# Attention and expert layer on one core: the experts' second product moved behind the two-level rounds

## The chip, the cores and the metric

The kernel runs on one core of a Trainium2 chip. The metric is the device time of one execution in microseconds; the median of several runs counts. The engines of the core are TensorE (PE), VectorE (DVE), ScalarE (ACT), GpSimd (POOL) and SyncE (SP), whose queue issues all DMAs of this kernel.

## The reference, cut to what matters

```python
x = hidden_states                                    # (2, 512, 512), float32
xn = layernorm(x)
out = x + attn(xn) + ffn(xn)

# attn: linear attention with decay, 32 heads of 128, over xn
#   q, k, v = silu(xn @ qkv_w.T);  gate = sigmoid(xn @ gate_w.T)
#   result  = (gate * rmsnorm(scan(q, k, v)) * norm_w) @ out_w.T

# ffn over the 1024 tokens of xn
logits  = xn @ W_router.T                            # 8 experts
combine = top-2 of softmax(logits), renormalised     # (1024, 8)
h       = einsum('nd,erd->ner', xn, A)               # rank 16 for each expert
hw      = h * combine[:, :, None]
ffn     = xn @ W_base.T + b_base + einsum('ner,eor->no', hw, B) * 2
```

What the change concerns is the last line: the base projection `xn @ W_base.T`, the bias, and the experts' second product with `B` (called `wlb` in the kernel, 128 rows of expert and rank by 512).

## The kernel before, in words

The 1024 tokens are eight tiles of 128 (NT = 8, four for each of the two sequences). Everything is float32. The kernel has these stages.

**Setup.** The eight tiles of x are loaded and normalised in four groups (L240 to L260). For each tile PE transposes xn into `xnT` (L252, bank "fr", copied by ACT at L253), multiplies it with the router and the experts' first weights (`wra`, bank "ra"), and ACT copies the logits `lg` and the experts' inner values `hl`. `base(t)` (L227) projects tile t with `wbase` into one of four banks `seeded` (sd0 to sd3, tile t uses t mod 4), and DVE adds the result to `x_sb[t]` (L233); it is called three tiles behind the transposes. Then DVE finds the two best experts of every token (L266 to L299) and scales `hl` by their weights (L300), forms the sums `xsum` of blocks of `xnT` (L306 to L309) and the second-level sums `xt` (L316 to L319). POOL adds the bias to `x_sb` (L321). PE transposes `hl` (L326), ACT copies it (`hT`, L329), PE multiplies with `wlb` (L333, recorded at the helper's line L80), DVE adds to `x_sb[t]` (L334), and the sum is stored in DRAM as `x_kept`.

**Two-level rounds.** The products that give v and the gate for all heads are done by a fast matrix multiplication scheme with seven products at two levels. `rounds` lists the outer products (n, q), seven for each of eight sets of weights n (four of v, four of the gate); each has seven inner products, whose slots are in `SLOTS`, two of them trailing one round behind. POOL makes the operands two rounds ahead: `encode` builds outer sums `s` (L177, a pool of 5 buffers) and inner sums `e` (L191 to L194, 3 buffers) from the raw weights. PE multiplies (L362, L366) into banks "fr" and the four `seeded`; DVE and ACT combine (L401 to L434) through temporaries of the pool `aw2` (`temp`: `z` with 6 buffers, `c` with 2); finished blocks go to DRAM (`v_kept`, `gate_kept`).

**First phase.** For each head the products for q and k (L488, one level), the attention (L550 to L589), and stores of gated heads.

**Second phase.** The output projection, in one level, with the first three pairs already worked in at the end of the first phase; at the end `x_kept` is read back, and the rows are finished and stored.

The order of the instructions on every engine is not written out by hand: a scheduler places the program's instructions in the engines' queues, and semaphores follow from the tiles. An engine works its queue in order. A pool's buffer is given out again when the last reader of its earlier tile is done. The pools `sp` (setup) and `aw2` share memory, as do the pools of the rounds and those of the first phase. The phase's PSUM banks ("ch", "sc", "at") take over the banks of the rounds.

Of the kernel before, what the change touches and what calls it, by code (L numbers as in the profile page):

```python
# [33 lines left out]
F32 = mybir.dt.float32  # L34
AF = mybir.ActivationFunctionType
ALU = mybir.AluOpType
# [4 lines left out]
P = 128  # L41
B, S, HID = 2, 512, 512
# [3 lines left out]
NT = B * TB  # L46
# [3 lines left out]
NE, R = 8, 16  # L50
# [9 lines left out]
def attn_moe_kernel(ctx: ExitStack, tc: tile.TileContext, x, qk_w, v_w, gate_w, out_w, norm_w,  # L60
                    decay, base_w, base_b, router_a_w, lora_b, out):
    nc = tc.nc
# [6 lines left out]
    dram = pool("dram", DRAM)  # L69
# [6 lines left out]
    def bank(tag):  # L76
        return ps.tile([P, 512], F32, tag=tag, name=f"ps_{tag}", bufs=banks[tag])

    def mm(o, lhsT, rhs, start, stop):
        nc.tensor.matmul(o, lhsT, rhs, start=start, stop=stop)  # L80
# [10 lines left out]

    v_kept, gate_kept = ([dram.tile([P, 2, HG, B, S], F32, tag=f"{n}_kept{i}", name=f"{n}_kept{i}")
                          for i in range(NG // 2)] for n in ("v", "gate"))
    x_kept = dram.tile([P, NT, HID], F32, tag="x_kept", name="x_kept")

    def inv_sqrt(sp, mean_sq, n, name, scale=None):

# [75 lines left out]
    def encode(n, q):  # L173

        def outer(k, a, b, op):
            t = sums2[n, k] = aw.tile([P, 2, 2, 256], F32, tag="s", name="s", bufs=5)
            nc.gpsimd.tensor_tensor(t, a, b, op)  # L177

        if q == 6:
            outer(1, raw_block(n, 1, 0), raw_block(n, 1, 1), ALU.add)  # L180
            outer(2, sums2[n, 1], raw_block(n, 0, 0), ALU.subtract)
        elif q == 7:
            outer(3, raw_block(n, 0, 0), raw_block(n, 1, 0), ALU.subtract)
        elif q == 3:
            outer(4, raw_block(n, 0, 1), sums2[n, 2], ALU.subtract)
        block = {1: lambda: raw_block(n, 0, 0), 2: lambda: raw_block(n, 0, 1), 3: lambda: sums2[n, 4],
                 4: lambda: raw_block(n, 1, 1), 5: lambda: sums2[n, 1], 6: lambda: sums2[n, 2],
                 7: lambda: sums2[n, 3]}[q]()
        a11, a12, a21, a22 = (inner(n, block, i, j) for i in range(2) for j in range(2))
        e = aw.tile([P, 4, 2, P], F32, tag="e", name="e", bufs=3)  # L190
        nc.gpsimd.tensor_tensor(e[:, 0], a21, a22, ALU.add)  # L191
        nc.gpsimd.tensor_tensor(e[:, 1], e[:, 0], a11, ALU.subtract)
        nc.gpsimd.tensor_tensor(e[:, 2], a11, a21, ALU.subtract)
        nc.gpsimd.tensor_tensor(e[:, 3], a12, e[:, 1], ALU.subtract)  # L194
        operand[n, q] = {1: a11, 2: a12, 3: e[:, 3], 4: a22, 5: e[:, 0], 6: e[:, 1], 7: e[:, 2]}

    rounds = []
# [3 lines left out]
    rounds.append((NSET - 1, 4))  # L201


    xt = [aw.tile([P, 4, S // 2], F32, tag=f"xt{q}", name=f"xt{q}") for q in range(1, 8)]
    with tc.tile_pool(name="setup", bufs=1) as sp:
        x_sb = [sp.tile([P, HID], F32, tag=f"x{t}", name=f"x{t}") for t in range(NT)]
# [1 line left out]
        nc.gpsimd.memset(ones, 1.0)  # L208
        wra = sp.tile([P, KC, NE + ER], F32, tag="wra", name="wra")
        wbase = sp.tile([P, KC, HID], F32, tag="wbase", name="wbase")  # L210
        wlb = sp.tile([P, HID], F32, tag="wlb", name="wlb")
        bias = sp.tile([P, HID], F32, tag="bias", name="bias")
        for t in range(NT):
            nc.sync.dma_start(x_sb[t], x[t * P : (t + 1) * P, :])
            if t == 2:
                nc.sync.dma_start(wra, router_a_w)
        nc.sync.dma_start(wbase, base_w)
        nc.sync.dma_start(bias, base_b.partition_broadcast(P))
        nc.sync.dma_start(wlb, lora_b)
        load_set(0)  # L220
        nc.sync.dma_start(nw, norm_w)
        load_set(1)
# [4 lines left out]
        def base(t):  # L227

            b, tt = divmod(t, TB)
            bp = seeded[t % 4]  # L230
            for c in range(KC):
                mm(bp, xnT[b][:, c, tt * P : (tt + 1) * P], wbase[:, c, :], c == 0, c == KC - 1)
            nc.vector.tensor_tensor(x_sb[t], x_sb[t], bp, ALU.add)  # L233


        lg = sp.tile([P, NT, NE], F32, tag="lg", name="lg")
        hl = sp.tile([P, NT, NE, R], F32, tag="hl", name="hl")
        stats = sp.tile([P, NT, 6], F32, tag="stats", name="stats")
        mv = sp.tile([P, NT, 2], F32, tag="mv", name="mv")
        for g, ts in enumerate(((0,), (1, 2), (3, 4, 5), (6, 7))):  # L240
            for t in ts:
                nc.vector.bn_stats(stats[:, t, :], x_sb[t])
                nc.vector.bn_aggr(mv[:, t, :], stats[:, t, :])
            rstd = inv_sqrt(sp, mv[:, ts[0] : ts[-1] + 1, 1], len(ts), f"ln{g}")
            for i, t in enumerate(ts):
                b, tt = divmod(t, TB)
                xn = sp.tile([P, HID], F32, tag="xn", name="xn", bufs=4)
                nc.vector.tensor_scalar(xn, x_sb[t], mv[:, t, 0:1], rstd[:, i : i + 1],
                                        ALU.subtract, ALU.mult)
                tp = bank("fr")  # L250
                for c in range(KC):
                    nc.tensor.transpose(tp[:, c * P : (c + 1) * P], xn[:, c * P : (c + 1) * P], ident)  # L252
                nc.scalar.copy(xnT[b][:, :, tt * P : (tt + 1) * P],  # L253
                               tp.rearrange("p (c s) -> p c s", c=KC))
                ra = bank("ra")
                for c in range(KC):
                    mm(ra[:, : NE + ER], xnT[b][:, c, tt * P : (tt + 1) * P], wra[:, c, :],
                       c == 0, c == KC - 1)
                nc.scalar.copy(lg[:, t, :], ra[:, :NE])
                nc.scalar.copy(hl[:, t].rearrange("p e r -> p (e r)"), ra[:, NE : NE + ER])  # L260
                if t > 2:
                    base(t - 3)
        for t in range(NT - 3, NT):
            base(t)

        prio = sp.tile([P, NT, NE], F32, tag="prio", name="prio")  # L266
        for e in range(NE):
# [50 lines left out]
            nc.vector.tensor_tensor(t[:, 2], i22, i12, ALU.subtract)  # L318
            nc.vector.tensor_tensor(t[:, 3], i21, t[:, 1], ALU.subtract)  # L319
        for t in range(NT):  # L320
            nc.gpsimd.tensor_tensor(x_sb[t], x_sb[t], bias, ALU.add)  # L321

        for q in range(NT // 4):
            tp = bank("fr")
            for i in range(4):
                nc.tensor.transpose(tp[:, i * P : (i + 1) * P],  # L326
                                    hl[:, q * 4 + i].rearrange("p e r -> p (e r)"), ident)
            hT = sp.tile([P, 4 * P], F32, tag="hT", name="hT", bufs=2)
            nc.scalar.copy(hT, tp)  # L329
            for i in range(4):  # L330
                t = q * 4 + i
                lp = seeded[i]
                mm(lp, hT[:, i * P : (i + 1) * P], wlb, True, True)  # L333
                nc.vector.tensor_tensor(x_sb[t], x_sb[t], lp, ALU.add)  # L334
                nc.sync.dma_start(x_kept[:, t, :], x_sb[t])

# [12 lines left out]
    def temp(tag, bufs=2):  # L351
        return aw2.tile([P, 512], F32, tag=tag, name=tag, bufs=bufs)

    def inner_product(o, r, i, first):
        n, q = rounds[r]
        a = operand[n, q][i]
        x_ = {1: xo[q][:, 0, :HB], 2: xo[q][:, 1, :HB], 3: xo[q][:, 1, HB:], 4: xt[q - 1][:, 3],
              5: xt[q - 1][:, 0], 6: xt[q - 1][:, 1], 7: xt[q - 1][:, 2]}[i]
        for u in range(2):
            if n % 2 == 0:  # L360
                for j in range(2):
                    nc.tensor.matmul(o[:, (2 * u + j) * P : (2 * u + j + 1) * P], x_[:, j * P : (j + 1) * P],  # L362
                                     a[:, u], start=first and u == 0 and j == 0, stop=True,
                                     skip_group_check=True)
            else:
                nc.tensor.matmul(o[:, u * HB : (u + 1) * HB], a[:, u], x_, start=first and u == 0, stop=True,  # L366
                                 skip_group_check=True)
# [18 lines left out]
    def after(r, i):  # L386
# [53 lines left out]
        elif i == 4:  # L440
            out_of(2, st["pd"])

    SLOTS = ((0, 1), (0, 5), (0, 2), (1, 7), (0, 6), (0, 3), (1, 4))
    for k in range(7 * len(rounds) + 7):
        r0, m = divmod(k, 7)
        if m == 0:
            if r0 + 2 < len(rounds):
                encode(*rounds[r0 + 2])
            if r0 < len(rounds):
                n, q = rounds[r0]  # L450
                state_of[r0] = {}
                for _, to in ADDED[q]:
                    if isinstance(to, str):
                        outer_sums[n, to] = aw2.tile([P, 4, 512], F32, tag="sum", name="sum", bufs=4)
                if q == 2 and 0 < n < NSET - 1:
                    load_set(n + 1)
                if (n, q) == (NSET - 1, 2):
                    load_pair(0)
                    for i in range(2):
                        load_unit(i)  # L460
        back, i = SLOTS[m]
        r = r0 - back
        if not 0 <= r < len(rounds):
            continue
        st = state_of[r]
        if i in (1, 5):
            st["pa" if i == 1 else "pc"] = bank("fr")
        inner_product(st[{1: "pa", 2: "pa", 5: "pc", 3: "pc", 6: "pb", 7: "pd", 4: "pd"}[i]], r, i, i in (1, 5))
        after(r, i)
    phase_a.close()  # L470


# [342 lines left out]
```

## Time and profile before

| | us |
|---|---|
| median of 3 runs | 1240.16 (1238.93 to 1240.45) |
| the profiled execution | 1241.71 |
| its span in the profile | 1239.9 |
| mean granted TensorE clock | 0.993 |

Busy in the stages, from the trace (us; PE, DVE, POOL):

| stretch | PE | DVE | POOL |
|---|---|---|---|
| 40 to 50 | 10.0 | 10.0 | 10.0 |
| 50 to 60 | 3.0 | 10.0 | 9.8 |
| 60 to 70 | 4.5 | 9.0 | 4.5 |
| 70 to 80 | 10.0 | 5.2 | 0.0 |
| 100 to 150 | 49.8 | 35.1 | 30.1 |
| 420 to 440 | 18.0 | 10.8 | 2.1 |
| 500 to 800 | 300.0 | 130.6 | 115.1 |

A line of a timeline gives start and length in us, the engine, the line of the kernel, the operation, what it writes and reads, shapes and count; in brackets stands the idle time of the engine before it and who released it. Matmuls in float32 leave two records each. PE's busy time is of records that overlap a little (a record holds the drain of the array too), so a row's length is a little more than what it adds to the row before.

### The profile page before, as it was taken

The numbers are of one execution on the slowest core, as the hardware profiler recorded it, in microseconds if no ns is written. First come the engines' busy times: TensorE is split into PE (matmuls) and PEld (weight loads), VectorE is DVE, ScalarE is ACT, GpSimd is POOL, SyncE is SP. The second block draws the span as 40 slices with busy tenths as digits, with TensorE's granted clock in tenths as the row PEclk, the third lists the DMA queues.
The fourth block names the chain that finished last, engine by engine and source line by source line (L and its number), as shares of the span: only waits on it lengthen the run. The fifth ranks groups of instructions, "written<-read, shape, count | busy, mean of one in ns | idle before, by whom it ended". The sixth has DMA issues, their size and how long they took to land.

```text
span 1239.9 us, 17100 instructions
## 1 busy us (share of the span) xinstructions
PE 1207.4 (97%) x6328; PEld 914.3 (74%) x6328; DVE 629.1 (51%) x1104; ACT 366.1 (30%) x648; POOL 592.8 (48%) x662
## 2 busy tenths in 40 slices
PE   6789999999999999999999999999999999999998
PEld 4369889899899745666666666666666669888887
DVE  5757666766766624444444434444444444455333
ACT  2124444444444422223222222222232332320000
POOL 3926568758756241434433433433333343655552
PEclk9989999999999999999999999999999999999999
DMA  8012543452442353343443443343334333843221
GB/s 315 0 68 75 173 151 121 153 170 96 161 161 103 123 166 91 119 135 112 145 140 103 125 134 102 117 125 118 116 114 128 120 97 108 309 150 122 93 92 52
DMA packets 102706, 158.17 MB, mean 128 GB/s; under 512 B 8800, under 2 KB 68192, under 8 KB 101344
## 3 DMA queue, kind: packets, MB, share of 16 engines
q1 hardware_dynamic: 102624, 157.09, 38.2%
q8 instruction: 50, 0.82, 0.3%
q14 instruction: 32, 0.26, 0.1%
HBM read 102.53 MB, written 54.53 MB: 127 GB/s over the span
## 4 chain that ended last, share of the span: by engine, by line
PE 93%; DVE 5%; issue 1%; ACT 1%; DMA 0%; SPq 0%; DVEq 0%; ACTq 0%
PE ps_ch L488 31%; PE ps_ch L645 9%; PE ps_at L80 8%; PE ps_sc L80 8%; PE ps_fr L362 7%; PE ps_fr L366 7%; PE sd L362 5%; PE sd L366 5%; PE ps_sc L645 4%; PE ps_at L645 2%; PE sd L80 2%; PE ps_sc L550 2%; DVE z L405 1%; DVE sum L405 1%; PE ps_ra L80 1%
## 5 line engine op out<-in xcount | busy, mean ns | idle before, releaser
L488 PE MATMUL ps_ch<-xsum,ws 128*128 128x512 f32 x384 | 180.0, 593 | 0.0
L562 POOL TENSOR_TENSOR qd<-q,mask 128x384 f32<-128x384 f32 x64 | 64.2, 1003 | 219.9 <-PE ps_at L80 214.8
L488 PE MATMUL ps_ch<-xnT,w 128*128 128x512 f32 x256 | 122.2, 600 | 0.8 <-DVE z L405 0.8
L488 PEld LDWEIGHTS ps_ch<-xsum,ws 128*128 128x128 f32 x384 | 68.5, 191 | 63.2 <-issue 63.2
L80 PEld LDWEIGHTS ps_at<-scores,v 128*128 128x128 f32 x512 | 77.4, 192 | 28.0 <-issue 27.7
L126 POOL TENSOR_TENSOR ws<-w 128x256 f32<-128x256 f32 x32 | 23.4, 730 | 154.3 <-DMA w<-in_qk_w 154.3
L503 DVE TENSOR_TENSOR c<-ps_ch,u 128x512 f32<-128x512 f32 x96 | 66.4, 691 | 58.4 <-PE ps_ch L488 58.4
L588 DVE SCALAR_TENSOR_TENSOR gT<-gate,ps_at 128x512 f32<-128x512 f32 x64 | 44.0, 687 | 97.5 <-ACT sq L585 94.5
L645 PE MATMUL ps_ch<-wsum,gsum 128*128 128x256 f32 x384 | 89.1, 379 | 0.0
L80 PE MATMUL ps_at<-scores,v 128*128 128x128 f32 x512 | 88.4, 275 | 0.0
L585 ACT ACTIVATE sq<-ps_at 128x512 f32<-128x512 f32 x62 | 37.0, 597 | 155.2 <-PE ps_at L80 155.1
L586 POOL TENSOR_TENSOR ssq<-ssq,sq 128x512 f32<-128x512 f32 x62 | 79.2, 1278 | 6.5 <-ACT sq L585 6.5
L645 PEld LDWEIGHTS ps_ch<-wsum,gsum 128*128 128x128 f32 x384 | 72.3, 190 | 9.5
L80 PE MATMUL ps_at<-qd,state 128*128 128x128 f32 x384 | 74.2, 275 | 0.0
L80 PEld LDWEIGHTS ps_sc<-v,kd 128*128 128x128 f32 x384 | 52.8, 191 | 28.4 <-issue 28.2
L633 POOL TENSOR_TENSOR wsum<-wo 128x256 f32<-128x256 f32 x32 | 25.3, 790 | 93.0 <-PE ps_ch L645 37.4
L488 PEld LDWEIGHTS ps_ch<-xnT,w 128*128 128x128 f32 x256 | 44.4, 192 | 34.2 <-issue 33.1
L503 DVE TENSOR_TENSOR u<-ps_ch,p 128x512 f32<-128x512 f32 x32 | 22.1, 692 | 91.4 <-PE ps_ch L488 85.5
L80 PE MATMUL ps_sc<-q,k 128*128 128x128 f32 x512 | 67.6, 275 | 0.0
L552 ACT ACTIVATE kd<-ps_sc,mask 128x384 f32<-128x384 f32 x64 | 37.2, 580 | 89.8 <-PE ps_sc L550 89.8
L626 DVE TENSOR_TENSOR gsum<-gated 128x256 f32<-128x256 f32 x32 | 15.1, 470 | 95.2 <-PE ps_sc L645 66.7
L80 PEld LDWEIGHTS ps_sc<-q,k 128*128 128x128 f32 x512 | 62.2, 192 | 0.0
(224 smaller groups left out, 2633.6 us busy)
## 6 DMA issues: line engine op xcount, KB each, us to landing
w<-in_qk_w SPq DMA_DIRECT2D x32, 512.0 KB, 4.1
v_kept<-z SPq DMA_DIRECT2D x64, 256.0 KB, 2.4
gate_kept<-z SPq DMA_DIRECT2D x64, 256.0 KB, 2.4
v<-v_kept SPq DMA_DIRECT2D x64, 256.0 KB, 2.6
gate<-gate_kept SPq DMA_DIRECT2D x64, 256.0 KB, 3.2
g_kept<-gT SPq DMA_DIRECT2D x64, 256.0 KB, 2.5
gated<-g_kept SPq DMA_DIRECT2D x32, 512.0 KB, 3.7
raw<-in_v_w SPq DMA_DIRECT2D x8, 1024.0 KB, 6.6
```

What stands on the lines that cost most here:

```text
L80: nc.tensor.matmul(o, lhsT, rhs, start=start, stop=stop)
L362: nc.tensor.matmul(o[:, (2 * u + j) * P : (2 * u + j + 1) * P], x_[:, j * P : (j + 1) * P], a[:, u], start=first and u == 0 and j == 0, st ...
L366: nc.tensor.matmul(o[:, u * HB : (u + 1) * HB], a[:, u], x_, start=first and u == 0, stop=True, skip_group_check=True)
L488: nc.tensor.matmul(o, a[:, c, :], b[:, c, :], start=first and c == 0, stop=c == 1, skip_group_check=True)
L503: nc.vector.tensor_tensor(o, p, t, ALU.add)
L552: nc.scalar.activation(kd.rearrange("p j d -> p (j d)"), pk[:, : (TB - 1) * P], AF.Copy, scale=mask[:, 0, P - 1 : P])
L562: nc.gpsimd.tensor_tensor(qd, q[:, P:].rearrange("p (j n) -> p j n", j=TB - 1), mask[:, 1, :].unsqueeze(1).to_broadcast([P, TB - 1, P]), A ...
L585: nc.scalar.activation(sq, pa, AF.Square)
L586: nc.gpsimd.tensor_tensor(ssq[b], ssq[b], sq, ALU.add)
L588: nc.vector.scalar_tensor_tensor(gT, gate.pop((head, b)), 1.0, pa, ALU.add, ALU.mult)
L633: nc.gpsimd.tensor_tensor(t[:, 0], b12, b11, ALU.subtract)
L645: nc.tensor.matmul(sums[n][:, i * HO : (i + 1) * HO], l[:, i * P : (i + 1) * P], r, start=p == 0 and i == 0, stop=p == NP - 1, skip_group_ ...
```

## The change

The experts' second product and the bias are taken out of the setup and done by a generator `experts()`, whose steps are called at the end of the rounds: it starts its loads in the last round, takes six steps in the two trailing slots after it, and the rest behind them. It works in the one bank "ra" and with temporaries of the rounds (`c` for `wlb` and the bias, `z` for the rows). For this the base projection with x added goes to DRAM as `x_base` and is loaded again tile by tile; `hl` moves to the pool `aw`, and the pool of `s` has 4 buffers in place of 5. The base projections are no longer called between the transposes, but behind them, at the end of the setup's code.

```diff
-    x_kept = dram.tile([P, NT, HID], F32, tag="x_kept", name="x_kept")
+    x_kept, x_base = (dram.tile([P, NT, HID], F32, tag=n, name=n) for n in ("x_kept", "x_base"))
...
-            t = sums2[n, k] = aw.tile([P, 2, 2, 256], F32, tag="s", name="s", bufs=5)
+            t = sums2[n, k] = aw.tile([P, 2, 2, 256], F32, tag="s", name="s", bufs=4)
...
+    hl = aw.tile([P, NT, NE, R], F32, tag="hl", name="hl")
...
-        nc.sync.dma_start(bias, base_b.partition_broadcast(P))
-        nc.sync.dma_start(wlb, lora_b)
...
             nc.vector.tensor_tensor(x_sb[t], x_sb[t], bp, ALU.add)
+            nc.sync.dma_start(x_base[:, t, :], x_sb[t])
...
-                if t > 2:
-                    base(t - 3)
-        for t in range(NT - 3, NT):
-            base(t)
...
         for t in range(NT):
-            nc.gpsimd.tensor_tensor(x_sb[t], x_sb[t], bias, ALU.add)
-
-        for q in range(NT // 4):
-            tp = bank("fr")
-            for i in range(4):
-                nc.tensor.transpose(tp[:, i * P : (i + 1) * P],
-                                    hl[:, q * 4 + i].rearrange("p e r -> p (e r)"), ident)
-            hT = sp.tile([P, 4 * P], F32, tag="hT", name="hT", bufs=2)
-            nc.scalar.copy(hT, tp)
-            for i in range(4):
-                t = q * 4 + i
-                lp = seeded[i]
-                mm(lp, hT[:, i * P : (i + 1) * P], wlb, True, True)
-                nc.vector.tensor_tensor(x_sb[t], x_sb[t], lp, ALU.add)
-                nc.sync.dma_start(x_kept[:, t, :], x_sb[t])
+            base(t)
...
+    def experts():
+
+        wlb, bias = temp("c"), temp("c")
+        nc.sync.dma_start(wlb, lora_b)
+        nc.sync.dma_start(bias, base_b.partition_broadcast(P))
+        yield
+        for q in range(NT // 4):
+            tp = bank("ra")
+            for i in range(4):
+                nc.tensor.transpose(tp[:, i * P : (i + 1) * P],
+                                    hl[:, q * 4 + i].rearrange("p e r -> p (e r)"), ident)
+            hT = aw2.tile([P, 4 * P], F32, tag="hT", name="hT", bufs=1)
+            nc.scalar.copy(hT, tp)
+            yield
+            for i in range(4):
+                t = q * 4 + i
+                o = temp("z", 6)
+                nc.sync.dma_start(o, x_base[:, t, :])
+                nc.vector.tensor_tensor(o, o, bias, ALU.add)
+                lp = bank("ra")
+                mm(lp, hT[:, i * P : (i + 1) * P], wlb, True, True)
+                nc.vector.tensor_tensor(o, o, lp, ALU.add)
+                nc.sync.dma_start(x_kept[:, t, :], o)
+                yield
+
+    last = experts()
...
         if m == 0:
+            if r0 == len(rounds) - 1:
+                next(last)
...
+        if r0 >= len(rounds):
+            for _ in range(3):
+                next(last, None)
         inner_product(st[{1: "pa", 2: "pa", 5: "pc", 3: "pc", 6: "pb", 7: "pd", 4: "pd"}[i]], r, i, i in (1, 5))
         after(r, i)
+    for _ in last:
+        pass
     phase_a.close()
```

More of the change, by code (lines that the diff above doesn't have):

```diff
@@ L210, in attn_moe_kernel @@
         wbase = sp.tile([P, KC, HID], F32, tag="wbase", name="wbase")
-        wlb = sp.tile([P, HID], F32, tag="wlb", name="wlb")
-        bias = sp.tile([P, HID], F32, tag="bias", name="bias")
         for t in range(NT):
@@ L233, in base @@
             nc.vector.tensor_tensor(x_sb[t], x_sb[t], bp, ALU.add)
+            nc.sync.dma_start(x_base[:, t, :], x_sb[t])
         lg = sp.tile([P, NT, NE], F32, tag="lg", name="lg")
-        hl = sp.tile([P, NT, NE, R], F32, tag="hl", name="hl")
         stats = sp.tile([P, NT, 6], F32, tag="stats", name="stats")
```

## The prediction

> **What bounds the kernel now.** I read the page's busy shares first, then PE's timeline at the two places that the change touches (the setup and the end of the two-level rounds), then DVE's and POOL's timelines of the setup. Parts 1 and 2 of the page:
>
> ```profile
> PE 1207.4 (97%) x6328; PEld 914.3 (74%) x6328; DVE 629.1 (51%) x1104; ACT 366.1 (30%) x648; POOL 592.8 (48%) x662
> PE   6789999999999999999999999999999999999998
> PEclk9989999999999999999999999999999999999999
> ```
>
> PE is busy for 97% of the span: only what gives PE less to do or closes a gap of its can pay. Only 32.5 us of the span are free of matmuls; the waits of PE put 11.0 before the first transpose and 12.5 in front of L326. PE's timeline of the setup (start, length, engine, line, operation, count, idle before):
>
> ```profile
> 39.99 13.04 PE L80 MATMUL sd<-wbase,xnT 128*128 128x512 f32 x30
> 65.51 1.97 PE L326 MATMUL ps_fr<-ident,hl 128*128 128x128 f32 x8 [12.48 <-DVE hl L300]
> 67.27 0.64 PE L362 MATMUL ps_fr<-raw,xnT 128*128 128x128 f32 x2
> 67.70 8.97 PE L80 MATMUL sd<-wlb,hT 128*128 128x512 f32 x16
> 76.50 0.83 PE L362 MATMUL ps_fr<-raw,xnT 128*128 128x128 f32 x6
> ```
>
> Base projections end at 53.0, PE waits for DVE's gated hl, does eight transposes and the experts' product, and starts the rounds at 76.5 (76.3, counting the two matmuls at 67.3). A logical f32 product is two records here. Warm, a 128x512 record takes 0.4347 us start to start (13.04 for 30); after the wait the sixteen wlb records took 8.8 instead of 6.95 us, because the granted clock was 0.50 until about 71.6. I put what the half clock cost from 65.5 on at 3.1 us: 6.8 us until 72.3 for work that warm takes 3.7.
>
> Why hl comes so late is in two timelines, first DVE's, then POOL's:
>
> ```profile
> 38.94 1.42 DVE L306 TENSOR_TENSOR xsum<-xnT,xnT 128x1024 f32<-128x1024 f32 x1 [0.36 <-ACT xnT L253]
> 44.29 3.38 DVE L309 TENSOR_TENSOR xsum<-xnT,xsum 128x1024 f32<-128x1024 f32 x1
> 64.24 1.21 DVE L300 TENSOR_TENSOR hl<-hl,hit 128x1024 f32<-128x1024 f32 x1
> 68.32 0.41 DVE L319 TENSOR_TENSOR xt<-xsum,xt 128x256 f32<-128x256 f32 x1
> ```
>
> ```profile
> 44.25 2.34 POOL L177 TENSOR_TENSOR s<-raw 128x1024 f32<-128x1024 f32 x1
> 46.55 1.70 POOL L194 TENSOR_TENSOR e<-s,e 128x256 f32<-128x256 f32 x1
> ```
>
> The two engines take turns. L309 starts at 44.29, ends at 47.67, that is 1.08 after POOL's L177 ended at 46.59; POOL's L194 then ends 0.58 after L309. So one turn of DVE is 1.08 us (1024 wide), about 0.28 (256) or 0.08 (64); one turn of POOL 2.22 (1024), 1.2 (512) or 0.58 (256).
>
> At the other end, PE's timeline:
>
> ```profile
> 429.06 1.03 PE L366 MATMUL sd<-xt,e 128*128 128x256 f32 x4
> 431.32 1.13 PE L366 MATMUL sd<-xt,raw 128*128 128x256 f32 x4 [1.23 <-DVE z L401]
> 433.24 3.66 PE L488 MATMUL ps_ch<-xnT,w 128*128 128x512 f32 x4 [0.78 <-DVE z L405]
> 436.69 5.38 PE L488 MATMUL ps_ch<-xsum,ws 128*128 128x512 f32 x12
> ```
>
> The rounds hand over to the first phase with only 2.0 us of gaps. The four records from 433.24 take twice their warm time: those gaps were enough to halve the clock from 433.4 to 436.8.
>
> **What the Trainium skill says.** "SBUF — State Buffer", section "SBUF: two separate sides", calls the port pair that VectorE and GpSimd share "an exclusive lock, not a bandwidth split", taken for a whole instruction, also by a DVE operation with two SBUF inputs; the turns above agree to 0.05 us. "TensorE: Matmul & The Clock Gate", Part 1 on the clock gate, gives a free-running window of 3.4 us: an idle one halves the clock, a busy one restores it. The trace agrees (half clock for 3.4 us from 433.4); a window with PE busy for 36% of it, 430.0 to 433.4, already sufficed, while one with about 48%, 156.9 to 160.4, left the clock alone. The same page, Part 4 on PE-mode transposes, says that transposes don't count as busy in the same way; the slow start at 65.5 fits, no run here shows it by itself.
>
> **Setup, what goes.** Eight transposes and sixteen wlb records leave PE (7.8 us warm, 10.6 as they ran), two hT copies ACT, eight bias adds POOL, eight L334 adds DVE, and the wlb and bias loads (0.5 MB) stand no longer ahead of the raw weights on SP's queue. At the 390 GB/s of that stretch POOL's encodes start 1.3 us earlier, at 18.5 instead of 19.80.
>
> **Setup, what moves.** Transposes are no longer interleaved with base projections. Tile 3's end at 17.9 as before; then a tile costs about 1.6 us (a router product 1.0, lg and hl copies 0.35, hops), so the last xnT is there near 24.8 instead of 38.9. Base projections of tiles 0 to 3 follow (32 records, 13.9, with two router products 2.0 between): PE is through at 39.9. Tile 4 writes bank sd0, so it waits for DVE's add of tile 0, and in the changed program's instruction order all eight base adds stand on DVE behind the top-2 chain, hl and nearly all xt. So PE's wait stays; the question is how long.
>
> That chain and POOL take turns from 18.5 on. POOL: 12 e operations and 8 ws at 0.58, 4 s at 2.22, 20.5 us. DVE: 28 xt at 0.28, 4 xsum at 1.08, hl 1.14, ten 64-wide at 0.08, 14.1 us; small ones and start-up 1.6. Sum: 18.5+20.5+14.1+1.6=54.7. Done for the kernel before, from 38.94, the same sum gives 70.8 where 68.7 was measured, so I take 54.0 for the end of tile 0's add. PE is then idle for 14 us (12.5 before). Tiles 4 to 7: 13.9, half clock at first 2.6 to 3.1. Rounds start at 54.1+13.9+2.9=70.9 to 71.5; taken 71.5 against 76.3: **4.8 us earlier**. Bounds: 9 earlier if DVE ends at 50, 2 if at 56.5.
>
> Eight x_base stores replace eight x_kept stores on SP; the last is issued as long after PE's last base record as the last x_kept store was after the last wlb record. The pool behind them (aw2) was first written at 80.61 without a visible DMA wait, so nothing. If one landed 2 us later, ACT's y copy and DVE's first sum would wait, and PE two slots on.
>
> Buffers of s go from 5 to 4: POOL's s for the second set, done at 44.25 before, now waits for a buffer that PE frees in round 3 or 5. From there to PE's first use lie 29 matmuls or more (6.5 us), POOL needs 2.34+0.73=3.1. Nothing; 2 either way, since DVE's SBUF adds in the rounds also meet POOL's s (a PE gap of 1.8 at 158.6 comes from that).
>
> **End of the rounds, what is added.** In the changed order PE does four hl transposes ahead of the last two slots, wlb product 0 between the last two, and then products 1, 2, 3, four transposes, products 4 to 7, all ahead of the first L488-type product. All use the one bank "ra", so each product waits until DVE has added the one before. One turn: 1.03 (two records with drain) + 0.04 + DVE 0.69 + 0.06 = 1.82 (L334 and L401 show these hops), less overlap 1.75. In the time of before: transposes at 429.06, product 0 at 430.4, product 1 at 432.7 behind the two DVE adds of tile 0, product 2 at 434.6, product 3 at 436.4, transposes at 438.2, hT copy 0.59, product 4 at 439.6, product 7 at 445.0, the first phase at 445.9 instead of 433.24: **12.7 us later**.
>
> DMAs: loads of x_base have 2.5 us each, and those of tiles 4 to 7 need z buffers that stores of tiles 0 to 2 and a gate result free; by the same replay they land 1.5 to 2 us before DVE needs them. Stores and loads stand alternately on SP's queue, behind them the next w loads (first used 27 us later) and v and gate (33 us later): covered. ACT's p1 copy needs the last store landed; the four open ch banks give PE 6.9 us, as they cover 5.2 now (438.45).
>
> Clock: PE is busy for about 47% of this stretch, and the window over the second transposes has 35 to 48%. If it stays warm, 1.7 us of half clock at 433.24 is saved, 11.0; if it drops at product 4, 12.7+3.4=16.1, up to 18 with late loads. I take 13.2.
>
> **Sum.** -4.8+13.2=+8.4. The profiled execution took 1241.71 (span 1239.9 and 1.8 around it), 1.55 above the median of 1240.16; set on the median: **1248.5 us**.
>
> **Rivals.** (a) The setup opens up, and the kernel gets faster. If DVE and POOL did not delay each other, tile 0's add would be there at about 42 (24.8+14.1+some), the base projections would run through almost without a gap and warm, and the rounds start at 56: 1240.2-20.3+13.2=1233. It decides from an add before about 46. Against it: every turn above. 8%. (b) The tail hides: if PE's products fell into gaps or overlapped, only 7.8 warm us less the 2.0 of gaps would be added, 1240.2-4.8+5.8=1241. For it: DVE and ACT have time there; against it: one bank and PE's fixed order. 10%. (c) The clock drops in the tail and loads are late: 18 in place of 13.2, 1253, and with a setup gain of 2 us only, 1256. 24%. My forecast, 1244 to 1251, 55%; 3% for what I don't see.
>
> **How the numbers follow.** About 0.2% (2.5 us) is what a measurement here can tell from no change. Faster by more: (a) and a little of (b), 0.10; within: most of (b), 0.08; slower: 0.82. From 1241, the middle of (b), to 1257, above (c), about 8 in 10 and somewhat more lie inside.
>
> **What would show it.** In the changed profile: an idle PE of 12 to 16 us in front of the fifth base projection, released by DVE's add of x0; rounds from about 71.5; at their end eight wlb products about 1.8 us apart on ps_ra, each released by DVE; granted clock below 1 there or not. Wrong, if tile 0's add ends before 46, if the wlb products stand closer than 1.5 us, or if a gap of several us opens in the rounds behind POOL's s.

## The result and the profile after

The changed kernel takes **1258.74 us** (median, 1258.03 to 1259.70) against 1239.56 for the kernel before (1238.93 to 1240.45, four runs; the table at the start has the median of three): 19.2 us slower, a ratio of 1.0155 (95% interval 1.0137 to 1.0172). The sign was right. The forecast of 1248.5 was 10.2 too low, and the time lies 1.7 above the range.

The profiled execution took 1258.03 with a span of 1256.2, so the two spans differ by 16.3. The other 2.9 of the 19.2 are no stage of the kernel: the profiled run of before lay 2.15 above its median, that of after 0.71 below its own.

Parts 1 and 2 of the page after (busy us with share and count; then tenths of PE busy and of granted clock in 40 slices):

```profile
PE 1215.3 (97%) x6328; PEld 914.3 (73%) x6328; DVE 636.2 (51%) x1112; ACT 365.5 (29%) x648; POOL 578.4 (46%) x654
PE   6599999999999899999999999999999999999998
PEclk9799999999999979999999999999999999999999
```

PE has exactly the records it had, 6328, and is busy 7.9 us longer. The clock row shows why that can be: a 7 stands in slice 15 (from 440 to 471), where before there was a 9. (The 7 in slice 2 is the wait in the setup; before, an 8 stood in slice 3 for it.) So the page alone says that at the end of the rounds PE ran at a lowered clock for part of the time. Four stretches of the trace after (window, length, busy us of PE, PEld, DVE, ACT, POOL with counts, granted clock, DMA share, GB/s) hold the whole difference:

```profile
0.00:70.90 70.90, 44.91 (x160) 26.17 (x161) 52.77 (x107) 10.27 (x31) 31.04 (x40) 0.88 0.43 156
70.90:424.30 353.40, 351.18 (x2345) 321.54 (x2344) 233.31 (x333) 159.91 (x285) 222.42 (x240) 1.00 0.38 130
424.30:449.00 24.70, 16.21 (x33) 5.59 (x31) 13.34 (x21) 3.48 (x6) 4.28 (x7) 0.72 0.79 258
449.00:1256.20 807.20, 802.95 (x3792) 561.02 (x3792) 336.80 (x652) 191.85 (x326) 320.68 (x368) 1.00 0.38 123
```

The same stretches of before are 76.30, 352.76, 4.18 and 806.66 long. So: setup -5.4, rounds +0.6, end of the rounds **+20.5**, the rest +0.5. In the third row, note that PE is busy for 66% of the time, at a clock of 0.72, while the DMA engines are 79% busy (48% in the same stretch of the kernel before).

PE's waits of after, without the one at the very start (waited for: us in total, times, longest):

```profile
PE sd L80 <- DVE x L230: 15.2, 1, 15.2
PE ps_ra L80 <- DVE z L443: 6.3, 6, 1.9
```

The 12.5 in front of the gated hl is gone, and a wait of 15.2 in front of the fifth base projection has its place. PE's timeline of the setup:

```profile
26.93 12.18 PE L80 MATMUL sd<-wbase,xnT 128*128 128x512 f32 x28
54.35 16.73 PE L80 MATMUL sd<-wbase,xnT 128*128 128x512 f32 x32 [15.24 <-DVE x L230]
70.91 1.05 PE L341 MATMUL ps_fr<-raw,xnT 128*128 128x128 f32 x8
```

And PE's timeline at the end of the rounds, the view that carries the loss (L80 here are the experts' products, two records each):

```profile
424.34 0.60 PE L431 MATMUL ps_ra<-ident,hl 128*128 128x128 f32 x4
...
425.64 1.10 PE L80 MATMUL ps_ra<-c,hT 128*128 128x512 f32 x2
...
429.03 1.12 PE L80 MATMUL ps_ra<-c,hT 128*128 128x512 f32 x2 [1.30 <-DVE z L443]
430.93 1.12 PE L80 MATMUL ps_ra<-c,hT 128*128 128x512 f32 x2 [0.78 <-DVE z L443]
433.94 1.12 PE L80 MATMUL ps_ra<-c,hT 128*128 128x512 f32 x2 [1.89 <-DVE z L443]
435.85 1.12 PE L431 MATMUL ps_ra<-ident,hl 128*128 128x128 f32 x4 [0.78 <-DVE z L443]
437.64 2.07 PE L80 MATMUL ps_ra<-c,hT 128*128 128x512 f32 x2 [0.67 <-ACT hT L434]
...
449.05 3.63 PE L500 MATMUL ps_ch<-xnT,w 128*128 128x512 f32 x4 [0.78 <-DVE z L443]
```

Three things are to be read here. An undisturbed turn is 1.12 + 0.78 = 1.90 us (429.03 to 430.93). One turn, 430.93 to 433.94, takes 3.01: its wait is 1.89 in place of 0.78. And from the second transposes on, every record takes nearly twice as long (2.07 for a product in place of 1.12), so that products 4 to 7 turn every 2.85 us. PE names DVE as the releaser each time; what DVE itself waited for is in DVE's timeline:

```profile
427.49 0.69 DVE L440 TENSOR_TENSOR z<-z,c 128x512 f32<-128x512 f32 x1 [0.95 <-DMA z<-x_base]
432.41 0.69 DVE L440 TENSOR_TENSOR z<-z,c 128x512 f32<-128x512 f32 x1 [0.93 <-DMA z<-x_base]
```

These are the bias adds of tiles 0 and 2, which held up products 1 and 3. A third, of tile 4 at 436.84, waited 1.04 for its load, but it did not hold PE: product 4 waited for ACT's `hT`.

### The profile page after: what moved, and what is told of

It is laid out like the page before. It is cut to its first block, busy times and chain, and to the rows that moved or that the text cites. A ratio compares the mean times of both kernels' runs of the same rounds, so it can differ in the third digit from the quotient of the medians.

```text
span 1256.2 us, 17135 instructions
## 1 busy us (share of the span) xinstructions
PE 1215.3 (97%) x6328; PEld 914.3 (73%) x6328; DVE 636.2 (51%) x1112; ACT 365.5 (29%) x648; POOL 578.4 (46%) x654
## 4 chain that ended last, share of the span: by engine, by line
PE 88%; DVE 8%; ACT 1%; DMA 1%; issue 1%; SPq 0%; DVEq 0%; ACTq 0%
PE ps_ch L500 31%; PE ps_ch L657 9%; PE ps_at L80 8%; PE ps_sc L80 8%; PE ps_fr L345 6%; PE ps_fr L341 6%; PE sd L345 4%; PE ps_sc L657 4%; PE sd L341 4%; PE ps_at L657 2%; DVE sum L384 2%; DVE z L384 2%; PE ps_sc L562 2%; PE sd L80 1%; PE ps_ra L80 1%
## 5 line engine op out<-in xcount | busy, mean ns | idle before, releaser
L80 PEld LDWEIGHTS ps_at<-scores,v 128*128 128x128 f32 x512 | 77.4, 192 | 28.0 <-issue 27.7
L80 PE MATMUL ps_at<-scores,v 128*128 128x128 f32 x512 | 88.4, 275 | 0.0
L80 PE MATMUL ps_at<-qd,state 128*128 128x128 f32 x384 | 74.2, 275 | 0.0
L80 PEld LDWEIGHTS ps_sc<-v,kd 128*128 128x128 f32 x384 | 52.8, 191 | 28.4 <-issue 28.2
L80 PE MATMUL ps_sc<-q,k 128*128 128x128 f32 x512 | 67.6, 275 | 0.0
L80 PEld LDWEIGHTS ps_sc<-q,k 128*128 128x128 f32 x512 | 62.2, 192 | 0.0
```

## Experiments

**Theory.** Beside PE's own work for the experts, three causes make the end of the rounds 20.5 us longer: turns on one bank, loads of x_base that land late, and a clock that the resulting gaps halve. The setup's gain is small because the base projections behind the transposes wait for VectorE. **Rivals**: the turns on one bank alone; the loads alone (they pace every product); a setup whose gain can't be larger, since VectorE's chain sets it wherever the projections stand.

| kernel | median us | ratio to before (95%) |
|---|---|---|
| the changed kernel | 1258.74 | 1.0155 (1.0137 to 1.0172) |
| experts left out | 1235.99 | 0.9970 (0.9958 to 0.9981) |
| x_base loaded early | 1251.08 | 1.0093 (1.0076 to 1.0110) |
| products in three banks | 1254.06 | 1.0113 (1.0098 to 1.0128) |
| PE kept busy in the gaps | 1252.77 | 1.0109 (1.0094 to 1.0124) |
| early load and three banks | 1244.65 | 1.0033 (1.0019 to 1.0046) |
| early load, steps spread over three rounds | 1245.11 | 1.0039 (1.0024 to 1.0054) |
| base ahead of the top-2 chain | 1246.54 | 1.0049 (1.0035 to 1.0062) |
| base between the transposes | 1244.44 | 1.0036 (1.0027 to 1.0045) |
| before, base behind the transposes | 1246.36 | 1.0043 (1.0028 to 1.0058) |
| before, no bias adds | 1232.42 | 0.9939 (0.9924 to 0.9955) |
| base ahead of the chain, steps spread | **1233.53** | **0.9946 (0.9934 to 0.9958)** |
| base between, steps spread | 1234.53 | 0.9954 (0.9937 to 0.9970) |

Before was run again beside each set of kernels; its medians were 1239.65, 1240.74, 1240.36 and 1240.59. Differences of medians below are against the changed kernel's 1258.74, unless another is named; as the median of before moved by up to 1.2 us from set to set, so much of such a difference can be chance. The start of the rounds moves too: over the seven traces with the changed kernel's setup it lies between 69.55 and 71.27.

### Where the loss sits: the experts left out

```diff
-            nc.sync.dma_start(x_base[:, t, :], x_sb[t])
+            nc.sync.dma_start(x_kept[:, t, :], x_sb[t])
...
-    last = experts()
...
```

> The changed kernel without its experts' tail: the generator is never called, so the experts' product and the bias are left out of the output, and the base projection is stored as x_kept at once; the setup is the changed one. Theory (the setup gained what was forecast, 5.4 us from trace to trace, and the loss is all in the tail): PE's wait in front of the fifth base projection stays near 15 us, rounds start near 70.9, the tail is that of the kernel before (about 4.2 us from the last slots to the first phase), and the time is about 1234 (1239.6 less 5.4). Rival (the changed setup also slows the rounds, through 4 buffers of s or the stores of x_base): time at or above 1239, with a longer stretch between the first and the last round.

Measured 1235.99, 3.7 below before and 2 above what was expected. PE's wait for x0 is still there at 14.9, and the stretch at the end of the rounds is 4.16 long, as before (4.18). So the loss is in the experts' steps at the end. In the trace the rounds start 6.3 earlier than before and take 2.0 longer, and the first phase's first records save 1.7, since they run at full clock here: what the setup gives is a few us, no more. Why the rounds take 2.0 longer here, and 0.6 in the changed kernel, was not followed up.

### Late loads: x_base loaded early

One load of all eight rows into a buffer of the raw weights that is free by then, issued with those of wlb and the bias in the fourth round from the end:

```diff
+        rows = aw.tile([P, 2, HG * KC * P], F32, tag="raw", name="rows", bufs=2).rearrange("p u (t f) -> p (u t) f", f=HID)
+        nc.sync.dma_start(rows, x_base)
...
-                o = temp("z", 6)
-                nc.sync.dma_start(o, x_base[:, t, :])
+                o = rows[:, t, :]
...
-            if r0 == len(rounds) - 1:
+            if r0 == len(rounds) - 4:
```

> The changed kernel with one load of all of x_base into a free buffer of raw weights, started some rounds earlier, instead of eight loads in the tail that wait for buffers of z. Theory (the tail is a chain over one bank; the loads added about 2 us of waiting, and the gaps that they made also brought the granted clock down): the waits of DVE for x_base go (0.95 and 0.93 us on the path), product turns stay 1.9 us apart while the clock is full; 1255 to 1257 if the clock falls all the same, about 1251 to 1252 if it does not. Rival (the loads set the pace of the tail): 1245 or less.

Measured 1251.08, 7.7 less than the changed kernel: the case in which the clock does not fall. PE's timeline of this run:

```profile
424.89 0.60 PE L433 MATMUL ps_ra<-ident,hl 128*128 128x128 f32 x4
...
430.50 1.12 PE L80 MATMUL ps_ra<-c,hT 128*128 128x512 f32 x2 [0.78 <-DVE rows L444]
...
443.31 1.98 PE L501 MATMUL ps_ch<-xnT,w 128*128 128x512 f32 x4 [0.78 <-DVE rows L444]
```

Every turn is now 1.90, and the granted clock over 424.89 to 443.31 is 1.00, up to the first phase, whose first four records take 1.98 in place of 3.63. With the loads gone from the stretch, the half clock is gone too, though the kernel does nothing for the clock itself. What is left, 18.42 from transposes to first phase, is the turns and PE's own work.

### Turns alone: three banks

```diff
-                lp = bank("ra")
+                lp = bank("fr")
```

> The changed kernel with the wlb products in the three fr banks in place of the one ra bank. Theory (one bank makes every product wait for DVE): products no longer alternate one for one with DVE's adds; what is left is DVE's two adds for each tile and the loads behind z; the first phase starts about 8 to 10 us earlier than in the changed kernel, 1249 to 1251. Rival (loads set the pace): unchanged within 2 us, 1257 to 1259.

Measured 1254.06: 4.7 less than the changed kernel, between the two forecasts, and neither hit. PE's waits of this run say what took the place of the turns:

```profile
PE ps_ch L500 <- DVE z L443: 4.4, 1, 4.4
PE ps_fr L80 <- DVE z L443: 4.1, 2, 2.6
```

PE runs ahead in the three banks, then waits 8.5 us for DVE, which waits for loads of x_base (6.4 us in four waits); the first phase begins 21.1 us after the first transposes. The clock fell here as well: the last two products take 3.78 for their four records and the first phase's first four 3.59. So three banks alone gain little, and the rival that the loads pace everything was too strong: 4.7 is not nothing.

### The clock: PE kept busy in the gaps

A throwaway product of the row before, which nobody reads, goes into bank "fr" behind each product from the second on, and one more behind the second transposes:

```diff
...
+                if prev is not None:
+                    mm(bank("fr"), prev[:, :P], wlb, True, True)
...
```

> The changed kernel with a throwaway product of the same size behind each wlb product from the second on and one behind the second transposes, into fr banks that nobody reads; it fills PE's wait for DVE. Work is added (eight products more), none is left out. Theory (four of the turns take 2.85 instead of 1.90 us only because the clock was halved in the gaps): turns of products 4 to 7 come down to about 1.9, the clock reads 1.00 through the tail, and the first phase starts warm: 3.8 and up to 1.7 us less, 0.9 more for the last throwaway product, 1253 to 1256. Rival (the clock is not what slows them): 1259 to 1263.

Measured 1252.77, 6.0 less, with *more* work for PE. In its trace the turns without a late load are 1.89 to 1.90 to the end and the first phase's records take 1.98, while three waits of 1.24, 1.60 and 1.63 remain, in front of products 1, 3 and 6; the end:

```profile
442.16 1.13 PE L80 MATMUL ps_ra<-c,hT 128*128 128x512 f32 x2 [1.63 <-DVE z L448]
...
446.10 1.98 PE L506 MATMUL ps_ch<-xnT,w 128*128 128x512 f32 x4
```

The half clock is therefore a cost of its own: with the late loads still there, keeping PE busy takes it away. How much it is worth is less clear than the 6.0. From the first transposes to the first phase the trace has 22.81 in place of 24.71, and the first phase's first four records save 1.65: 3.6 together. Of the 5.1 between the two spans another 1.4 lies in the setup, which the edit does not touch. The stretch gains no more because PE at full clock catches up with the loads: the wait of 1.63 in front of product 6 is not there in the changed kernel.

### Two causes together, and the steps spread

Early load and three banks in one kernel:

> Both edits at once: wlb products in the three fr banks, and x_base loaded in one piece some rounds earlier. Theory (two things each bind the tail, so that taking either away alone uncovers the other: one bank, 1.90 us a turn, and loads behind buffers of z): now only DVE's sixteen adds of about 0.6 us bind, PE has no wait longer than about 1.5 us, the tail takes about 13 us from the hl transposes to the first phase, and the time is about 1245 to 1247. Rival (the two gains are the same gain): 1250 to 1252, as with the early loads alone.

Measured 1244.65, a little below what was expected: 14.1 less, more than the 7.7 and 4.7 of the two edits added. Its PE timeline has eight records of four products without a wait between:

```profile
426.30 3.70 PE L80 MATMUL ps_fr<-c,hT 128*128 128x512 f32 x8 [0.33 <-ACT hT L436]
...
431.16 3.70 PE L80 MATMUL ps_fr<-c,hT 128*128 128x512 f32 x8
...
435.65 1.98 PE L501 MATMUL ps_ch<-xnT,w 128*128 128x512 f32 x4 [0.78 <-DVE rows L444]
```

The stretch is 11.15 long, 7.0 more than the 4.18 of before: about PE's own work for the experts (7.8 warm, by the prediction's reckoning; part of it can lie in the gaps that were there). Each of the two edits alone had run into the other's wait.

So the traces split the 20.5, if the causes are taken away in this order: 4.2 for the clock and 2.1 for the late loads (24.71 down to 18.42 with the early load; the split is worked out in the section on the prediction), 7.3 for the turns (18.42 down to 11.15 with three banks as well), and 7.0 for PE's own work (11.15 down to 4.18). In another order the shares of clock and loads come out otherwise, as the run with the throwaway products shows.

The other way to take the turns away is to give them cover. The load is early, `wlb` and the bias go into a buffer of `s`, the bank stays one, and a step is taken at every other slot of the last three rounds; the last part of the edit:

```diff
...
-        if r0 >= len(rounds):
-            for _ in range(3):
-                next(last, None)
+        if len(rounds) - 3 <= r0 < len(rounds) and m % 2 == 0:
+            next(last, None)
...
```

> The changed kernel with the early load and the generator's steps called at every other slot of the last three rounds instead of behind them; still one bank. wlb and the bias go into a free buffer of s. Theory (what the tail costs over its 7.8 us of PE work is only waits, and other products of the rounds can stand in them): no wait on ps_ra above 0.3 us, the end of the rounds as in the kernel before, the time that of the version without experts plus 7.8: 1243 to 1245. Rival (DVE, which adds in the same place, becomes the bound and delays the rounds): 1248 or more.

Measured 1245.11, 13.6 less. PE has no visible wait on "ra" left; one of 1.2 for POOL's s and the 1.2 and 0.8 at the end of the rounds, which before had as well, are what remains. The version without experts is 9.1 faster (1235.99): about PE's own 7.8 and the wait for s.

### The setup: where the base projections stand

Ahead of the top-2 chain in the code, directly behind the transposes:

> The changed kernel with one call moved: the loop of base projections stands behind the transposes but ahead of the top-2 chain, so that DVE's adds of the base projections stand between the steps of that chain and not behind it; the tail is the changed one. Theory (PE's 15 us wait in front of the fifth base projection comes only from the place of DVE's adds): that wait goes, base projections end near 51 to 53, PE then meets the end of DVE's chain in the first round (about 57, and the last x_base store about 2.5 us later) and has effectively gained about 13 to 15 us; 1244 to 1246. Rival (DVE's and POOL's turns are the bound whatever the order, since the rounds wait for the same chain): 1255 to 1259.

Measured 1246.54, 12.2 less and 0.5 above what was expected. PE's timeline of this run:

```profile
46.91 12.26 PE L80 MATMUL sd<-wbase,xnT 128*128 128x512 f32 x24 [4.04 <-DVE x L230]
59.01 1.05 PE L341 MATMUL ps_fr<-raw,xnT 128*128 128x128 f32 x8
```

DVE's adds now stand between the steps of its chain, not behind it; PE waits 4.0 in place of 15.2, and the rounds start 11.9 earlier. Between the transposes again, as in the kernel before:

```diff
+                if t > 2:
+                    base(t - 3)
+        for t in range(NT - 3, NT):
+            base(t)
...
-        for t in range(NT):
-            base(t)
```

> The changed kernel with the base projections between the transposes again, as in the kernel before; experts' product and tail as changed. My theory: TensorE runs through its setup without the wait of 15 us, ends the base projections near 53, and then waits for VectorE's sums xt, which come out at 62 to 66 since the base adds stand early in its queue: the rounds start 5 to 9 us earlier than in the changed kernel, 1249 to 1254. Rival: the sums come no earlier than now and the rounds start at 69 to 72, 1257 to 1260: the place of the projections costs nothing. A second rival: nothing holds the rounds back and they start at 54 to 57, 1243 to 1245.

Measured 1244.44: 14.3 less, the second rival. Its rounds start at 51.38, while DVE still works on the sums, with one wait of 2.2:

```profile
58.26 1.44 PE L342 MATMUL ps_fr<-e,xnT 128*128 128x128 f32 x8 [2.25 <-ACT y L402]
```

I had put the end of DVE's sums at 62 to 66; it was 57.3, only 2.7 later than in the changed kernel (54.6). And the same placing done alone, in the kernel before:

> The kernel before with one edit: the base projections are called behind all transposes, as in the changed kernel; the experts' second product stays in the setup. My theory (VectorE's adds of the base projections then stand behind the top-2 chain and the sums, the fifth projection waits for a bank some 14 us, and the product with the gated hl, ready before, has to follow or lies in that wait): the experts' product can fill a part of the wait, so the rounds start within 3 us of the kernel before: 1238 to 1244, most likely 1242. Rival: the place costs the whole of the second wait, the kernel takes 1247 or more. A second rival: the place itself brings the setup's gain, 1235 or less.

Measured 1246.36, 6.0 more than before, between my range and the rival. PE's waits show what my reasoning missed:

```profile
PE sd L80 <- DVE x L233: 18.0, 1, 18.0
```

I had let the experts' product fill a part of the wait. In its timeline the transposes of hl come at 73.62, behind all base projections, in PE's fixed order, though hl was ready at 55.2: nothing fills the 18.0. The first of the rounds' rows behind the experts' products stands at 81.87, where before had 76.50.

### What the bias adds cost the kernel before

GpSimd's eight bias adds taken out:

> The kernel before without GpSimd's eight bias adds, so the bias is left out of the result. My theory (five of the adds take turns of 1.2 us each with VectorE's chain between 48 and 64, so the gated hl comes 6 us earlier): 1232 to 1236, TensorE's wait 6 to 7 instead of 12.5. Rival (the chain on VectorE alone sets hl, GpSimd's adds fill its gaps): 1239 or more, the wait stays at 12. A further one: half of it, 1236 to 1238.

Measured 1232.42, 8.2 below before. PE's wait of before on DVE's hl, 12.5 there, is in this run

```profile
PE ps_fr L323 <- DVE hl L300: 5.9, 1, 5.9
```

so half of that wait came from POOL's bias adds, whose results DVE's chain does not read. With the exclusive lock of the port pair that the Trainium skill describes ("SBUF — State Buffer", section "SBUF: two separate sides"), the five bias adds that lie between 48 and 64 would cost five turns of 1.2 us, by the prediction's price from the trace: an estimate of 6.0, and 6.6 were measured. Another 0.7 is the clock behind a shorter gap (the sixteen wlb records take 8.1 in place of 8.8); the last 0.9 were not traced.

### A version that beats both

The two halves mended together: base projections ahead of the top-2 chain, the load early, and the steps spread.

> Both remedies: base projections ahead of the top-2 chain, experts' steps in the last three rounds with the early load. Theory: the gains add up, about 14 us from the setup and about 15 from the tail against the changed kernel, 1229 to 1232, faster than the kernel before. Rival: the setup's gain is given back in the first rounds, 1236 to 1241.

Measured 1233.53, 0.5% below before, its interval clear of 1; 1.5 above what was expected, and below the rival. The two gains add: 12.2 + 13.6 = 25.8 off 1258.74 gives 1232.9. Its clock row has no dip:

```profile
PEclk9999999999999999999999999999999999999999
```

With the base projections between the transposes instead:

> The changed kernel with the base projections between the transposes again and with the experts' loads and steps spread over the last three rounds. My theory (the two parts add, -14.3 and -13.6 from 1258.74): 1229 to 1233. Rival: both recoveries are of the same idle time, and the kernel stays at 1237 or more.

Measured 1234.53, 1.5 above what was expected and 3.7 above the full sum of the two gains (1230.8): they did not quite add here. There is no clear difference to the other version, whose interval overlaps. The wait at the start of the rounds was 3.0 here in place of 2.2 in the run without the spreading, and PE began the rounds 1.2 later; why was not followed up.

## Why the prediction was right and wrong

**The setup was right, in mechanism and size.** "I take 54.0 for the end of tile 0's add": it ended at 54.29. "PE is then idle for 14 us": 15.24. "Rounds start at 70.9 to 71.5": 70.91; the gain of 4.8 was 5.4. The turns of DVE and POOL added up to 54.7, and from POOL's true start, 17.92 in place of 18.5, they give 54.1: the lock is a good model of this stretch. A hit to the tenth is luck all the same: the seven traces with this setup differ by 1.7.

**The terms put at nothing in the rounds held.** The rounds are 0.6 longer and the part behind them 0.5, and PE's waits there show none on POOL's s. ACT did wait 1.4 us for the last x_base store, which the prediction named as possible; PE shows no wait for it. The pool of s and the stores were not tested by themselves.

**The end of the rounds was wrong in size: +13.2 predicted, +20.5 measured.** The mechanism was right: products on one bank, each released by DVE. The failed step is the sum of this tail: it took the loads of x_base as there in time and the clock as mostly warm, and let the first phase start too soon. By the prediction's own replay the stretch from the transposes to the first phase is 16.84 (429.06 to 445.9); it is 24.71. With the early load it is 18.42, which splits the 7.9:

- *"Product 7 at 445.0, the first phase at 445.9."* With the early load 1.90 lie between the two (441.41 to 443.31), a whole turn: the first phase waits 0.78 for DVE's last add. The prediction's own line at 433.24 showed the same wait of 0.78. That is 1.0 too little. The turns themselves, 1.90 and not 1.75 to 1.82, and the second transposes make up the rest: 18.42 - 16.84 = 1.6.
- *"Loads of x_base have 2.5 us each", and those of tiles 4 to 7 land in time.* Here a load took 3.2 to 4.3, with a median of 3.9, and DVE waited for those of tiles 0, 2 and 4; for tiles 0 to 3 the prediction shows no replay. In the changed kernel product 3 starts 9.60 after the first transposes, with early loads 7.52: 2.1. SP's queue has a part in it: five stores of gate results go out between 418.56 and 423.9, directly ahead of the first load, and three more ahead of tile 2's:

```profile
426.12 1.87 SPq L362 DMA_DIRECT2D gate_kept<-z  x3
428.05 0.66 SPq L439 DMA_DIRECT2D z<-x_base  x1
```

  From 417 to 437 SP waited 5.2 us in front of stores of gate results, for ACT, and in front of no load of x_base: so by the profile these loads were held by the order of the queue and the time to land, not by a buffer.
- *The clock, counted with +0.5.* It fell to 0.50 at 435.3 and stayed there until 452.4, so products 4 to 7 and the second transposes cost 6.29 - 2.1 = 4.2 more than warm. The prediction had priced "drops at product 4" at 3.4 and named 18 with late loads as rival (c). That was what happened; 24% for it was too little, and its size was 2.5 short.

1.6 + 2.1 + 4.2 = 7.9. The three are not independent: the late loads open the gaps and the gaps halve the clock, since the early load ends both, and at full clock more of the loads come late. Rival (c) had the two together; the forecast itself put the loads at nothing and the clock at a half us, each for itself, and so missed that one causes the other.

Two readings of the prediction were off, without weight for the sum. In the 3.4 us from 430.0 to 433.4 PE was busy for 1.38, 41% and not 36%; and the 0.4347 for a record holds a share of the last one's drain (twelve records of the first phase step by 5.15, 0.429 each).

**The rivals.** (a), the setup opens up: not in the changed kernel, but the two runs with the projections elsewhere show that it was the place that held it shut. Without the move, the first phase starts at 434.19, 14.9 earlier than in the changed kernel. So taking the experts out of the setup frees about 20 us, and the move of the base projections takes about 15 of them back (14.3 by the medians; 11 to 12 where the steps are spread, 1245.11 against 1234.53 and 1233.53). Their placing alone could not show that in the kernel before (6.0), as the wait for hl was there already. (b), the tail hides: only the first product lay among the rounds' last slots, the others came where no more work of the rounds was left to cover a turn. Spread over three rounds, the turns did hide, and the experts cost 9.1 (1245.11 - 1235.99), little more than PE's own work.

What stays open: at which busy share the clock falls, and how much the place of the gaps matters. All four timed runs of the changed kernel had a mean clock of 0.983 to 0.986, against 0.992 to 0.995 with the early load, so it seems to have fallen in each of them; one was traced.

## What to carry to other kernels

Before a step is moved behind a loop, count the turns that it takes through one buffer, bank and queue: eight turns of 1.90 us made the end of the rounds 14 us longer even with every load there (18.4 in place of 4.2, half of it PE's own work), and among the work of three rounds little more than PE's own work remained. Where a stretch becomes a chain of short waits, ask first whether PE's busy share then halves the clock, and price late loads and lost clock as one case. And look at each of two edits that come together by itself: here undoing the one that seemed only to follow from the other gave back 14 of the 19 us.

## What the runs showed of the hardware

- **A clock once halved can stay halved.** The Trainium skill ("TensorE: Matmul & The Clock Gate", Part 1 on the clock gate) says that the clock comes back after a busy window of about 3.4 us. In the changed kernel it was 0.50 from 435.34 to 452.40, that is 17.06 us or five times 3.41, which agrees with windows of that length. If their borders lie there, PE was busy for 65, 77, 73 and 61% of the first four, and the clock stayed down; it came back behind the fifth, in which the first phase kept PE busy for 98%. The second and the fifth:

```profile
438.75:442.16 3.41, 2.63 (x4) 0.50 (x2) 1.29 (x2) 0.00 (x0) 0.00 (x0) 0.50 0.50 169
448.99:452.40 3.41, 3.35 (x4) 1.51 (x5) 0.01 (x1) 0.00 (x0) 1.31 (x2) 0.50 0.25 90
```

- **What the fall needs.** In the 3.41 us ahead of the fall, from 431.93 to 435.34, PE was busy for 1.25 (37%). With early loads the same turns, 1.12 busy of 1.90 (59%), left the clock at 1.00, also in the 3.4 us from 431.7 to 435.1, in which PE was busy for 1.78 (52%). So at half clock shares up to 77% did not bring the clock back, while at full clock 52% did not lower it. That the clock follows the busy share alone is not shown: what counts as busy for it is not in the trace.
- **Throwaway work can pay.** Products whose results nobody reads made the kernel 6.0 us faster by the medians; 3.6 of that are seen in the trace where they stand.
- **Loads beside stores.** The eight loads of x_base, 256 KB each, took 3.2 to 4.3 us to land, with a median of 3.9, while the DMA engines were about 80% busy. The gate results stored among them had a median of 2.9.
